# A windowed-attention block with a mixture of experts: the feed-forward's first product as seven block products, its other sums on other engines, and three seams in another order

## The chip, the cores and the metric

The kernel runs on one core of a Trainium2 chip. Five engines work side by side, each through its own queue in order: TensorE (PE, matmuls; PEld is its weight load), VectorE (DVE), ScalarE (ACT), GpSimd (POOL, which also issues the gathers by index) and SyncE (SP, which issues the other transfers). They meet through semaphores only. TensorE writes PSUM, of which the kernel keeps seven banks in one rotating pool and one bank apart. The metric is the time of one execution on the device in microseconds (us), as the median of several.

## The reference

Inputs are 4096 rows `x` of 256 numbers, and everything is float32. Cut to what matters (`LN` is a plain layer norm, biases are shown):

```python
xn   = LN(x)
# attention in windows of 64, 8 heads, each window sees itself and both neighbours
attn = window_attention(xn @ Wq + bq, xn @ Wk + bk, xn @ Wv + bv) @ Wo + bo
x1   = LN(xn + attn) * gamma + beta
mlp  = x1 + gelu(x1 @ W1 + b1) @ W2 + b2            # hidden width 1024
# mixture of experts: 8 experts, the two with the largest scores for each row
w    = top2_normalised(softmax(xn @ gate_w.T + gate_b))
moe  = sum_e w[e] * (silu((xn @ gp_w[e].T + gp_b[e]) * (xn @ up_w[e].T + up_b[e])) @ down_w[e].T + down_b[e])
out  = x + mlp + moe
```

## The kernel before

The whole program is one straight list of instructions: with `manual_schedule` every engine gets its instructions in the order in which the Python code emits them, and an engine whose next instruction waits holds everything behind it.

Stages, in order of time:

1. **Norm, scores, routing** (to about 75 us). The normed rows go to DRAM as `xnd`. Each row's two experts and its two places in the sorted list of (row, expert) pairs are worked out; `token` says which row belongs to each place, `slot` where each row's two results will lie.
2. **The main loop** `for b in range(ALWAYS)`, 34 rounds. Each round handles one *unit* of an expert's work (one or two tiles of 128 rows) and, in the first 32, one half of the heads for two tiles of the attention. A unit's rows come by `gather` (indirect transfers on GpSimd, L814), its weights by `load_gu` and `load_down` (SP, L214 and L222, 1670 KB and 896 KB). The expert's number is read from a table in SBUF: `expert_then`, a copy that GpSimd makes (L1326), for the units 0 and 1 once `gus` isn't empty, and `expert` otherwise. `turned` transposes the rows on TensorE (L827). The unit's results go to DRAM as `done` (L1003). In round `b == STEPS` (32) the attention's SBUF is given back, the feed-forward's weights `W1`, `W2` and the first two groups' inputs are loaded; in round 33 GpSimd makes `V2`, sums of blocks of `W2`; ScalarE's root and VectorE's few small steps make `r2` and `shift2` out of the second layer norm's moments, and `second_norm` (L1177) applies them to groups 0 and 1 late in the round.
3. **Late units** (to 850.72 us). Five more units may be needed or not; each lies in a `tc.If` on a flag (L1506), and `whole` computes it, with its copies from PSUM (`summed`, L985) at the end of the same branch. In this data three of the five run. Every engine goes through the branches, also those that have nothing in them.
4. **The feed-forward loop** `for g in range(NG)`, eight groups of 512 rows. `hidden(g)` makes x1 @ W1 on TensorE (L1210: eight banks of 512 columns, two products each) and ScalarE's Gelu out of PSUM into `hT` (L1217). `second(g - 1)`, one group behind, makes gelu(...) @ W2 out of seven products of blocks (L1281), with sums of hidden blocks (`sums_of_hidden`, VectorE, L1241 to L1245) and sums of weights (`V2`) as operands, and adds what comes out into `acc` on VectorE (L1291, L1301, L1309; u is ScalarE's copy of the first product, L1294). `turned2` transposes the next group's x1 (L1197) and ScalarE writes it to `x2T` (L1200). `second_base` puts x + beta + b2 + x2 * gamma into `acc` (VectorE, L1188 to L1190, 1024 wide). `picked` gathers the experts' results by row (L1255, eight transfers a group) and `combined` adds them to `acc`, weighted with `share` (VectorE, L1268, eight operations of 256). `store` writes `acc` out.

The seven products, here and below, are Winograd's form of Strassen's scheme: a product of 2 x 2 blocks with seven block products in place of eight, and fifteen block sums.

Of the kernel before, what the change touches and what calls it, by code (L numbers as in the profile page):

```python
# [103 lines left out]
def block_kernel(ctx: ExitStack, tc: tile.TileContext, a: dict, out: bass.AP):  # L104
# [24 lines left out]
    def bank(name):  # L129
        return psm.tile([P, G], F32, tag="bank", name=name)  # L130
# [873 lines left out]

    def whole(b, w, wd, xT, hT, banks, gss, y):

        _, n, _ = UNITS[b]
        n_in = n * P
        for k, f in enumerate([FCM] + list(range(FCM))):
            pb = halves(banks[k % 3])[:, :, 0:n_in]  # L1010
            gs = gss[k % 3][:, 0:n_in]
            if f == FCM:
                rest_of(w, xT, hT, pb, gs)
            else:
                chunk_of(f, w, xT, hT, pb, gs)
            if f == FCM:
                silu_rest(hT)
            elif f % 2:
                silu(hT, f - 1, f + 1)
        pds = [banks[k][:, 0:D] for k in (3, 1)[:n]]  # L1020
        results_rest(pds, wd, hT)
        results(pds, wd, hT)
        summed(y, pds)

# [140 lines left out]

    def second_loads(g):
        acc = accp.tile([P, TG, D], F32, tag="acc", name=f"acc{g}")
        x2 = accp.tile([P, TG, D], F32, tag="x2", name=f"x2_{g}", bufs=2)
        nc.sync.dma_start(out=x2, in_=rows(x1d, g * TG, TG))
        nc.sync.dma_start(out=acc, in_=rows(a["x"], g * TG, TG))  # L1170
        return acc, x2

# [12 lines left out]
    def second_base(g, acc, x2):  # L1185

        scaled = accp.tile([P, TG, D], F32, tag="scaled", name=f"scaled{g}", bufs=1)
        nc.vector.tensor_tensor(acc, acc, bcast(beta_b2, TG, 1), ALU.add)  # L1188
        nc.vector.tensor_tensor(scaled, x2, bcast(gamma, TG, 1), ALU.mult)
        nc.vector.tensor_tensor(acc, acc, scaled, ALU.add)  # L1190

# [12 lines left out]

    def hidden(g, x2T):
        hT = hf.tile([P, FC1, G], F32, tag="hf", name=f"hf{g}")
        for f in range(FC1):
            ph = bank(f"ph{g}_{f}")
            for c in range(DC):
                nc.tensor.matmul(  # L1210
                    ph,
                    W1[:, c, f * P : (f + 1) * P],
                    x2T[:, c, :],
                    start=(c == 0),
                    stop=(c == DC - 1),
                )
            nc.scalar.activation(hT[:, f, :], ph, AF.Gelu, bias=b1[:, f : f + 1])  # L1217
        return hT
# [30 lines left out]
    def picked(g):  # L1249

        ys = []
        for i in range(g * TG, (g + 1) * TG):
            for k in range(2):
                y = got.tile([P, D], F32, tag="got", name=f"got{i}_{k}")
                nc.gpsimd.indirect_dma_start(  # L1255
                    out=y,
                    out_offset=None,
                    in_=done,
                    in_offset=bass.IndirectOffsetOnAxis(ap=slot[:, k, i : i + 1], axis=0),
                )  # L1260
                ys.append(y)
        return ys

    def combined(g, acc, ys):
        for n, y in enumerate(ys):
            t, k = n // 2, n % 2
            i = g * TG + t
            nc.vector.scalar_tensor_tensor(  # L1268
                acc[:, t, :], y, share[:, k, i : i + 1], acc[:, t, :], ALU.mult, ALU.add
            )  # L1270

    def second(g, acc, hT, v):
# [31 lines left out]
        p5 = product(5, v[:, 0], V2[:, 0])  # L1304
        add(t1, C2, p5)
        add(t2, C2, p5)
        yield
        p7 = product(7, v[:, 2], V2[:, 2])
        nc.vector.tensor_tensor(u, p7, u, ALU.add)  # L1309
        add(t2, C1, u)  # L1310
        add(t2, C2, u)
        yield
# [10 lines left out]
    xs = {0: gather(0)}  # L1323
    res = {0: residual_load(0)}

    nc.gpsimd.tensor_copy(expert_then, expert)  # L1326
    downs[0], gus[1] = load_down(0), load_gu(1)
    xs[1] = gather(1)

# [24 lines left out]
    for b in range(ALWAYS):  # L1354
# [11 lines left out]
        if b == 0:  # L1366
            xT[0] = turned(0, xs.pop(0))
        if attends:
            pr, nm, sums = scores(i, hq)
            xd = apart(i, hq)  # L1370
# [40 lines left out]
        if b == STEPS:  # L1411
            att.close()
            wf = pool(ctx, "wf", right)
            accp = pool(ctx, "accp", right, bufs=4)
            V2 = wf.tile([P, 4, FC1 // 2, P], F32, tag="V2", name="V2")
            W1, W2 = matrix(wf, "W1", F1, DC), matrix(wf, "W2", D, FC1)
            b1 = column("b1", FC1, wf)
# [9 lines left out]
            for n in range(ALWAYS, BLOCKS):  # L1427
                xs[n] = gather(n)
            x2s = {n: second_loads(n) for n in range(2)}
        if b == STEPS + 1:  # L1430
            sums_of_weights()
            *_, r2 = rstd_of(mv2, root_of(mv2, NT, "b"), NT, "b")
            nc.vector.scalar_tensor_tensor(shift2, mv2[:, :, 0], -1.0, r2, ALU.mult, ALU.mult)
            nc.vector.tensor_tensor(beta_b2, beta, b2, ALU.add)
        if b == ALWAYS - 1:
# [3 lines left out]
        if b + 1 < ALWAYS:  # L1439
            xT[b + 1] = turned(b + 1, xs.pop(b + 1))  # L1440
        else:
            for n in range(ALWAYS, BLOCKS):
                xT[n] = turned(n, xs[n])
            for n in range(2):
                second_norm(n, x2s[n][1])
        g = b // TG
# [46 lines left out]

    x2Ts = {n: turned2(n, x2s[n][1]) for n in range(2)}

    for b in range(ALWAYS, BLOCKS):
        nc.gpsimd.memset(xs[b], 0.0)
    last = hTs[(ALWAYS - 1) % 2][:, :, 0 : UNITS[ALWAYS - 1][1] * P]
    pds = down_rest(ALWAYS - 1, downs[ALWAYS - 1], last)
    list(down(ALWAYS - 1, pds, downs.pop(ALWAYS - 1), last))  # L1500
    load_unit(ALWAYS + 2)
    for b in range(ALWAYS, BLOCKS):
        at, n, _ = UNITS[b]
        banks = [bank(f"whole{b}_{k}") for k in range(4)]
        gss = [he.tile([P, B], F32, tag="gs", name=f"gs{b}_{k}", bufs=3) for k in range(3)]
        with tc.If(flags[b] > 0):  # L1506
            whole(b, gus[b], downs[b], xT[b], hTs[b % 2][:, :, 0 : n * P], banks, gss, xs[b])
        load_unit(b + 3)

        nc.sync.dma_start(out=rows(done, at, n), in_=xs.pop(b))  # L1510

# [3 lines left out]
    hf = pool(ctx, "hf", right, bufs=2)  # L1515
    got = pool(ctx, "got", right, bufs=8)
    second_base(0, *x2s[0])
# [6 lines left out]
    for g in range(NG):  # L1524
        if g + 2 < NG:
            x2s[g + 2] = second_loads(g + 2)
        hT = hidden(g, x2Ts.pop(g))
        if g + 1 < NG:
            second_base(g + 1, *x2s[g + 1])
        if g > 0:  # L1530
            acc = x2s.pop(g - 1)[0]
            combined(g - 1, acc, ys)
        if 0 < g < NG - 1:
            x2Ts[g + 1] = turned2(g + 1, x2s[g + 1][1])
        if g + 2 < NG:
            second_norm(g + 2, x2s[g + 2][1])
        ys = picked(g)
        outs = second(g - 1, acc, *last) if g > 0 else iter(())
# [8 lines left out]
    acc = x2s.pop(NG - 1)[0]  # L1547
    combined(NG - 1, acc, ys)
    outs = second(NG - 1, acc, *last)
    some(outs, 6)  # L1550
    store(NG - 1, 0, 2, acc)
# [88 lines left out]
```

## Time and profile before

| | |
|---|---|
| runs | 1069.36, 1069.93, 1071.85 us; median 1069.93 us |
| profiled execution: its own time | 1071.19 us |
| profiled execution: span from first to last instruction | 1069.5 us |
| granted TensorE clock, mean | 0.998 |
| busy share of the span: PE, DVE, ACT, POOL | 99%, 70%, 54%, 55% |
| feed-forward loop, first matmul | 850.55 us (the chain counts it from 850.72) |
| one period of that loop, 945.79 to 972.91: PE, DVE, ACT, POOL busy | 27.12, 15.86, 9.05, 7.95 us of 27.12 |
| last operation on VectorE in the chain, then the last store | starts 1065.92, 0.42 us; span ends 1069.5 |

Times in all views are us from the start of the span. A line of a timeline has start, length, engine, line of the kernel, operation, and the tiles as written<-read; in brackets stands the idle time just before, and what ended it. In a table by groups of instructions a line ends with busy us, mean ns of one, and idle us before them.

### The profile page before, as it was taken

Reading aid. Unit: us, or ns where it says so; the run is one execution under the profiler, and the core shown is the slowest. Engines: PE = TensorE matmul, PEld = TensorE weight load, DVE = VectorE, ACT = ScalarE, POOL = GpSimd, SP = SyncE. Lnnn points to the kernel's source line nnn. Section 1 sums busy time; section 2 is a strip of 40 time slices with the busy share of each in tenths; the row PEclk is TensorE's granted clock in tenths of the full one; section 3 lists DMA queues with packets and bytes.
Section 4 is the critical chain, followed back from the end, with each engine's and each line's share of the span. In section 5 each row is a group of like instructions: output and inputs, shape, how many; then the busy total and the mean of one; then the engine's idle time right before and its main releaser. Section 6 shows DMA issues by size and latency. Waiting matters only on the chain. (4 is left out here: it accounts for less than half of the span.)

```text
span 1069.5 us, 20380 instructions
## 1 busy us (share of the span) xinstructions
PE 1057.4 (99%) x7278; PEld 860.8 (80%) x7278; DVE 753.9 (70%) x1852; ACT 572.6 (54%) x1329; POOL 587.8 (55%) x706
## 2 busy tenths in 40 slices
PE   9998999999999999999999999999999999999998
PEld 6577887887888888888888888888887757777778
DVE  6666876886787687788888988888532455555546
ACT  4526556656657556756675666566455353333320
POOL 5417766676576666676877777767520053222220
PEclk9999999999999999999999999999999999999999
DMA  8225434445345344544544444345584343333111
GB/s 287 75 102 204 139 129 173 172 150 180 118 143 183 129 146 165 199 139 143 177 175 139 176 158 181 138 167 173 187 310 145 123 137 114 99 99 96 63 60 40
DMA packets 61047, 158.67 MB, mean 148 GB/s; under 512 B 6576, under 2 KB 46896, under 8 KB 56208
## 3 DMA queue, kind: packets, MB, share of 16 engines
q1 hardware_dynamic: 53632, 139.33, 37.4%
q0 software_dynamic: 6480, 17.70, 5.2%
q8 instruction: 59, 0.97, 0.4%
q10 hardware_dynamic: 832, 0.30, 0.1%
q14 instruction: 44, 0.36, 0.1%
HBM read 135.43 MB, written 21.89 MB: 147 GB/s over the span
## 5 line engine op out<-in xcount | busy, mean ns | idle before, releaser
L839 PE MATMUL gu<-xsT,wg 128*128 128x256 f32 (+1 forms) x1632 | 364.4, 370 | 0.0
L839 PEld LDWEIGHTS gu<-xsT,wg 128*128 128x128 f32 x1632 | 290.0, 191 | 46.5 <-DVE nm L1047 8.6
L1255 POOL DMA_INDIRECT got<-done,slot x64 | 64.6, 1010 | 177.0 <-DVE acc L1268 106.8
L847 ACT ACTIVATE gs<-gu,wg 128x256 f32<-128x256 f32 (+1 forms) x204 | 92.2, 452 | 120.4 <-PE gu L839 116.0
L1074 POOL TENSOR_TENSOR pr<-pr 128x256 f32<-128x256 f32 x128 | 114.2, 892 | 67.0 <-ACT pr L1062 67.0
L848 DVE SCALAR_TENSOR_TENSOR hT<-gu,wg,gs 128x256 f32<-128x256 f32 (+1 forms) x204 | 91.9, 461 | 78.7 <-ACT gs L847 77.8
L1075 POOL TENSOR_TENSOR pr<-pr,ident 128x256 f32<-128x256 f32 x128 | 132.8, 1037 | 10.0
L1062 ACT ACTIVATE pr<-pr,nm 128x256 f32<-128x256 f32 x256 | 126.8, 497 | 1.0 <-ACT xsT L831 0.6
L1210 PE MATMUL ph<-x2T,W 128*128 128x512 f32 x256 | 111.0, 592 | 0.0
L1217 ACT ACTIVATE hf<-ph,b 128x512 f32<-128x512 f32 x64 | 43.9, 687 | 121.8 <-PE ph L1210 55.3
L1047 DVE CUSTOM_DVE_ANT_0 pr<-ps,mask 128x256 f32<-128x256 f32 x256 | 90.7, 421 | 16.6 <-PE ps L1033 16.6
L880 ACT ACTIVATE hT<-hT 128x512 f32<-128x512 f32 (+2 forms) x179 | 84.9, 485 | 32.5 <-DVE hT L848 22.4
L814 POOL DMA_INDIRECT xs<-xnd,token x71 | 69.0, 972 | 50.5 <-DVE paired_tiles L781 33.1
L1210 PEld LDWEIGHTS ph<-x2T,W 128*128 128x128 f32 x256 | 48.2, 190 | 57.9 <-issue 54.5
L1092 DVE TENSOR_TENSOR pr<-pr,rec 128x1024 f32<-128x1024 f32 x32 | 39.2, 1226 | 41.9 <-POOL pr L1074 41.9
L1105 POOL TENSOR_TENSOR xd<-xd,same 128x256 f32<-128x256 f32 x32 | 19.7, 617 | 83.7 <-DVE same L1103 83.5
L1291 DVE TENSOR_TENSOR acc<-u,acc 128x256 f32<-128x256 f32 x32 | 12.9, 423 | 68.7 <-ACT u L1294 68.1
L929 POOL TENSOR_TENSOR ts<-wd 128x384 f32<-128x384 f32 x54 | 54.1, 1001 | 2.1
L1062 ACT ACT_TABLE_LOAD x31 | 39.8, 1283 | 19.9 <-DVE nm L1047 19.9
L973 ACT COPY y<-sh 128x512 f32<-128x512 f32 x27 | 15.8, 586 | 61.4 <-PE sh L952 61.4
L1062 ACT ACTIVATION_READ_ACCUMULATOR pr<-pr,nm 128x1 f32 x256 | 48.3, 189 | 0.0
L952 PE MATMUL pe<-wd,hT 128*128 128x128 f32 x324 | 44.9, 275 | 0.0
(252 smaller groups left out, 2112.1 us busy)
## 6 DMA issues: line engine op xcount, KB each, us to landing
wg<-in_gate_up SPq DMA_DIRECT2D x37, 1670.5 KB, 7.1
wd<-in_down SPq DMA_DIRECT2D x37, 896.0 KB, 4.8
done<-y SPq DMA_DIRECT2D x30, 256.0 KB, 2.1
x<-in_x SPq DMA_DIRECT2D x8, 512.0 KB, 5.5
xnd<-xn SPq DMA_DIRECT2D x8, 512.0 KB, 5.2
res<-xnd SPq DMA_DIRECT2D x16, 256.0 KB, 2.9
x1d<-res SPq DMA_DIRECT2D x16, 256.0 KB, 2.2
x<-x1d SPq DMA_DIRECT2D x8, 512.0 KB, 4.6
```

Source lines behind the costliest of these rows:

```text
L814: nc.gpsimd.indirect_dma_start(out=x[:, t, :], out_offset=None, in_=xnd, in_offset=bass.IndirectOffsetOnAxis(ap=token[:, i : i + 1], axis=0),)
L839: nc.tensor.matmul(pb[:, k, :], w[:, lo : lo + P], xT[:, c, :], start=(c == 0), stop=(c == DC - 1),)
L847: nc.scalar.activation(gs, pb[:, 0, :], AF.Identity, bias=w[:, gb : gb + 1])
L848: nc.vector.scalar_tensor_tensor(hT[:, f, :], pb[:, 1, :], w[:, ub : ub + 1], gs, ALU.add, ALU.mult)
L880: nc.scalar.activation(hT[on, lo:hi, :], hT[on, lo:hi, :], AF.Silu)
L929: nc.gpsimd.tensor_tensor(out_, left_, right_, ALU.subtract)
L1047: nc.vector.tensor_tensor_reduce(out=pr[:, hh, j, :], in0=ps[hh][:, j, :], in1=mask[:, kinds[j], :], scale=-1.0, scalar=-LOWEST, op0=ALU.a ...
L1062: nc.scalar.activation(pr[:, hh, j, :], pr[:, hh, j, :], AF.Exp, bias=nm[:, j, hh : hh + 1], scale=-1.0, accum_out=sums[:, j, hh : hh + 1],)
L1074: nc.gpsimd.tensor_tensor(first, first, second, ALU.add)
L1075: nc.gpsimd.tensor_tensor(second, second, bcast(ident, 2, 1), ALU.mult)
L1210: nc.tensor.matmul(ph, W1[:, c, f * P : (f + 1) * P], x2T[:, c, :], start=(c == 0), stop=(c == DC - 1),)
L1255: nc.gpsimd.indirect_dma_start(out=y, out_offset=None, in_=done, in_offset=bass.IndirectOffsetOnAxis(ap=slot[:, k, i : i + 1], axis=0),)
```

## The change

It has four parts.

- **First product.** `hidden` makes, for each of four pairs of 128 hidden columns, seven products of 256 columns out of blocks of `W1` and `x2T` and their sums: `V1` (four sums of weight blocks, made once on GpSimd behind `V2`) and `x2s` (four sums of input blocks for each group, GpSimd). The seven results lie in four banks. ScalarE copies p1 into `q`, VectorE makes five sums into `hT`, and the Gelus work in place on `hT`, out of SBUF. Behind them stands one step of `weighted`.
- **Other sums.** `second_base` moves from VectorE to GpSimd, in pieces of 256. The weighting with `share` moves from VectorE's `combined` to ScalarE (`weighted`: two scalings behind each block of `hidden`), and `combined` becomes two sums of 1024. `picked` is called right behind `hidden`. In `second` two pairs of adds become one add each.
- **Rows and norms.** `gather(1)` moves ahead of the copy `expert_then` and the loads that read it. The rows x2 of groups 0 and 1 are loaded ahead of `W1`; root, `shift2`, `beta_b2` and `second_norm` for both move to the start of round 33.
- **Late units' copies.** A unit's copies out of PSUM and its store move into a branch of their own, `emptied`, which is emitted behind the next unit's `whole`; the same holds for the copies of the last unit of the main loop.

```diff
@@ late units
-    def whole(b, w, wd, xT, hT, banks, gss, y):
+    def whole_results(b, banks):
+        return [banks[k][:, 0:D] for k in (3, 1)[: UNITS[b][1]]]
+
+    def whole(b, w, wd, xT, hT, banks, gss):
...
         results(pds, wd, hT)
-        summed(y, pds)
+
+    def emptied(b, banks, y):
+        at, n, _ = UNITS[b]
+        with tc.If(flags[b] > 0):
+            summed(y, whole_results(b, banks))
+
+        nc.sync.dma_start(out=rows(done, at, n), in_=y)
+        yield
@@ second_base
-        nc.vector.tensor_tensor(acc, acc, bcast(beta_b2, TG, 1), ALU.add)
-        nc.vector.tensor_tensor(scaled, x2, bcast(gamma, TG, 1), ALU.mult)
-        nc.vector.tensor_tensor(acc, acc, scaled, ALU.add)
+        for t in range(TG):
+            a_, s_ = acc[:, t, :], scaled[:, t, :]
+            nc.gpsimd.tensor_tensor(s_, x2[:, t, :], gamma, ALU.mult)
+            nc.gpsimd.tensor_tensor(a_, a_, beta_b2, ALU.add)
+            nc.gpsimd.tensor_tensor(a_, a_, s_, ALU.add)
@@ hidden
+    def sums_of_first_weights():
+        m = blocks_of_first()
+        a11, a12, a21, a22 = m[:, 0, 0], m[:, 0, 1], m[:, 1, 0], m[:, 1, 1]
+        s1, s2, s3, s4 = (V1[:, k] for k in range(4))
+        nc.gpsimd.tensor_tensor(s1, a21, a22, ALU.add)
+        for out_, left_, right_ in ((s2, s1, a11), (s3, a11, a21), (s4, a12, s2)):
+            nc.gpsimd.tensor_tensor(out_, left_, right_, ALU.subtract)
+
+    def sums_of_inputs(g, x2T):
+        ts = turns.tile([P, 4, B], F32, tag="x2s", name=f"x2s{g}")
+        b11, b12, b21, b22 = x2T[:, 0, 0:B], x2T[:, 0, B:], x2T[:, 1, 0:B], x2T[:, 1, B:]
+        t1, t2, t3, t4 = (ts[:, k] for k in range(4))
+        for out_, left_, right_ in ((t1, b12, b11), (t2, b22, t1), (t3, b22, b12), (t4, b21, t2)):
+            nc.gpsimd.tensor_tensor(out_, left_, right_, ALU.subtract)
+        return x2T, ts
+
-    def hidden(g, x2T):
+    def hidden(g, x2T, ts, others):
         hT = hf.tile([P, FC1, G], F32, tag="hf", name=f"hf{g}")
-        for f in range(FC1):
-            ph = bank(f"ph{g}_{f}")
-            for c in range(DC):
-                nc.tensor.matmul(ph, W1[:, c, f * P : (f + 1) * P], x2T[:, c, :], ...)
-            nc.scalar.activation(hT[:, f, :], ph, AF.Gelu, bias=b1[:, f : f + 1])
+        w = blocks_of_first()
+        for m in range(FC1 // 2):
+            banks = [halves(bank(f"ph{g}_{m}_{k}")) for k in range(4)]
+            p1, p6, p7, p5, p2, p4, p3 = (banks[k // 2][:, k % 2, :] for k in range(7))
+            for to, left_, right_ in (
+                (p1, w[:, 0, 0, m, :], x2T[:, 0, 0:B]),
+                (p6, V1[:, 1, m, :], ts[:, 1]),
+                (p7, V1[:, 2, m, :], ts[:, 2]),
+                (p5, V1[:, 0, m, :], ts[:, 0]),
+                (p2, w[:, 0, 1, m, :], x2T[:, 1, 0:B]),
+                (p4, w[:, 1, 1, m, :], ts[:, 3]),
+                (p3, V1[:, 3, m, :], x2T[:, 1, B:]),
+            ):
+                nc.tensor.matmul(to, left_, right_, start=True, stop=True)
+
+            q = hf.tile([P, 3, B], F32, tag="q", name=f"q{g}_{m}")
+            both = hT[:, 2 * m : 2 * m + 2, :]
+            nc.scalar.copy(q[:, 0], p1)
+            nc.vector.tensor_tensor(q[:, 1], p6, q[:, 0], ALU.add)
+            nc.vector.tensor_tensor(q[:, 2], p7, q[:, 1], ALU.add)
+            nc.vector.tensor_tensor(both[:, :, B:], q[:, 1:3], bcast(p5, 2, 1), ALU.add)
+            nc.vector.tensor_tensor(both[:, :, 0:B], banks[2], q[:, 0::2], ALU.add)
+            nc.vector.tensor_tensor(both[:, 0, B:], p3, both[:, 0, B:], ALU.add)
+            for f in range(2 * m, 2 * m + 2):
+                nc.scalar.activation(hT[:, f, :], hT[:, f, :], AF.Gelu, bias=b1[:, f : f + 1])
+            next(others, None)
         return hT
@@ picked, combined
-                y = got.tile([P, D], F32, tag="got", name=f"got{i}_{k}")
+        ys = got.tile([P, 2, TG, D], F32, tag="got", name=f"got{g}")
...
-            nc.vector.scalar_tensor_tensor(
-                acc[:, t, :], y, share[:, k, i : i + 1], acc[:, t, :], ALU.mult, ALU.add
-            )
+    def weighted(g, ys):
+        for t in range(TG):
+            for k in range(2):
+                i = g * TG + t
+                nc.scalar.activation(
+                    ys[:, k, t, :], ys[:, k, t, :], AF.Copy, scale=share[:, k, i : i + 1]
+                )
+            yield
+
+    def combined(acc, ys):
+        for k in range(2):
+            nc.vector.tensor_tensor(acc, acc, ys[:, k], ALU.add)
@@ second
-        add(t1, C2, p5)
-        add(t2, C2, p5)
+        right = acc.rearrange("p (k t) d -> p k t d", k=2)[:, :, :, C2]
+        nc.vector.tensor_tensor(right, right, bcast(p5, 2, 1), ALU.add)
...
-        add(t2, C1, u)
-        add(t2, C2, u)
+        low = acc[:, t2, :].rearrange("p t (h n) -> p t h n", h=2)
+        nc.vector.tensor_tensor(low, low, bcast(u, 2, 2), ALU.add)
@@ rows
     res = {0: residual_load(0)}
+    xs[1] = gather(1)
     nc.gpsimd.tensor_copy(expert_then, expert)
     downs[0], gus[1] = load_down(0), load_gu(1)
-    xs[1] = gather(1)
@@ norms, at the start of round STEPS + 1 (before: behind its second chunk, second_norm behind the transposes)
+        if b == STEPS + 1:
+            *_, r2 = rstd_of(mv2, root_of(mv2, NT, "b"), NT, "b")
+            nc.vector.scalar_tensor_tensor(shift2, mv2[:, :, 0], -1.0, r2, ALU.mult, ALU.mult)
+            nc.vector.tensor_tensor(beta_b2, beta, b2, ALU.add)
+            for n in range(2):
+                second_norm(n, x2s[n][1])
@@ the late units
+    x2Ts = {n: sums_of_inputs(n, x2T) for n, x2T in x2Ts.items()}
...
-    list(down(ALWAYS - 1, pds, downs.pop(ALWAYS - 1), last))
+    made = down(ALWAYS - 1, pds, downs.pop(ALWAYS - 1), last)
+    next(made)
...
+        list(made)
+        made = emptied(b, banks, xs.pop(b))
         load_unit(b + 3)
-        nc.sync.dma_start(out=rows(done, at, n), in_=xs.pop(b))
+    list(made)
@@ the feed-forward loop
-        hT = hidden(g, x2Ts.pop(g))
+        hT = hidden(g, *x2Ts.pop(g), weighted(g - 1, ys) if g > 0 else iter(()))
+        ys_last = ys if g > 0 else None
+        ys = picked(g)
         if g + 1 < NG:
             second_base(g + 1, *x2s[g + 1])
-        if g > 0:
-            acc = x2s.pop(g - 1)[0]
-            combined(g - 1, acc, ys)
         if 0 < g < NG - 1:
-            x2Ts[g + 1] = turned2(g + 1, x2s[g + 1][1])
+            x2Ts[g + 1] = sums_of_inputs(g + 1, turned2(g + 1, x2s[g + 1][1]))
         if g + 2 < NG:
             second_norm(g + 2, x2s[g + 2][1])
-        ys = picked(g)
+        acc = x2s.pop(g - 1)[0] if g > 0 else None
+        if g > 0:
+            combined(acc, ys_last)
         outs = second(g - 1, acc, *last) if g > 0 else iter(())
@@ the last group
-    combined(NG - 1, acc, ys)
+    list(weighted(NG - 1, ys))
     outs = second(NG - 1, acc, *last)
-    some(outs, 6)
+    some(outs, 2)
+    combined(acc, ys)
+    some(outs, 4)
```

## The prediction

> **What bounds the kernel now.** I read the granted clock first (0.998), then the page, then the chain of work that ended last in order of time, then each engine's timeline over one period of the feed-forward loop and over the three seams. The chain:
>
> ```profile
> 918.68 13.74 PE ph L1210 x32
> 932.41 0.87 PE pt L1197 x8
> 933.29 12.51 PE s L1281 x112
> 945.79 13.73 PE ph L1210 x32
> ...
> 1040.88 25.02 PE s L1281 x224
> 1065.90 0.02 issue
> 1065.92 0.42 DVE acc L1291
> ```
>
> Columns: start, length (us), engine, tile, line. From 850.72 on TensorE alone carries the end: a period is 13.74 (`hidden`) + 0.87 (`turned2`) + 12.51 (`second`) = 27.12 us, without idle. From 850.72 to the end of the span are 1069.5 - 850.72 = 218.8 us; that is the number the change is held against. The other engines are slack there, and this is how one of them is ordered:
>
> ```profile
> 909.21 0.36 ACT L1294 COPY u<-s 128x256 f32<-128x256 f32 x1
> 920.48 0.69 ACT L1217 ACTIVATE hf<-ph,b 128x512 f32<-128x512 f32 x1 [10.91 <-issue]
> 922.15 0.69 ACT L1217 ACTIVATE hf<-ph,b 128x512 f32<-128x512 f32 x1 [0.98 <-PE ph L1210]
> ```
>
> Each Gelu waits for TensorE alone, and nothing on ScalarE waits behind VectorE. Ahead of the loop TensorE stands still at two places that the change touches (in brackets: idle time, releaser):
>
> ```profile
> 86.88 0.55 PE L827 MATMUL pts<-ident,xs 128*128 128x128 f32 x3 [2.92 <-DMA xs<-xnd,token]
> 806.84 1.03 PE L889 MATMUL pe<-wd,hT 64*128 64x256 f32 x4 [1.28 <-ACT hT L880]
> ```
>
> **TensorE's own part.** `hidden` had 16 products of 512 columns, in 32 instructions of 13.74 / 32 = 0.429 us. Now it has 4 blocks of 7 products of 256 columns, 56 instructions. Such instructions at L839 come 24 in 5.18 us (777.11 to 782.29), 0.216 each: 56 x 0.216 = 12.09 us a group, 3.02 a block. Taken alone, 8 x 1.65 = 13.2 us less. Weight loads (0.19 us at L1210) fit under 0.216.
>
> **The new queue on ScalarE.** This decides. In each block ScalarE copies p1 into q, VectorE runs five sums, ScalarE runs two Gelus and, from group 1 on, two scalings of gathered rows. The instruction order of the changed kernel puts the copy of the next block *behind* the Gelus of this one, and those wait for VectorE's fifth sum. So copy, sums, Gelus and scalings run one after the other, however early TensorE is. Prices:
>
> ```profile
> 912.87 0.42 DVE L1301 TENSOR_TENSOR u<-s,u 128x256 f32<-128x256 f32 x1
> 913.32 0.42 DVE L1291 TENSOR_TENSOR acc<-u,acc 128x256 f32<-128x256 f32 x1
> ...
> 760.66 0.68 DVE L1114 TENSOR_TENSOR pr<-pT,first_keys 128x512 f32<-128x512 f32 x1
> 761.26 0.68 DVE L1114 TENSOR_TENSOR pr<-pT,second_keys 128x512 f32<-128x512 f32 x1
> ...
> 808.16 0.63 ACT L880 ACTIVATE hT<-hT 128x512 f32<-128x512 f32 x1 [0.55 <-DVE hT L848]
> 808.70 2.77 ACT L1200 ACTIVATE x2T<-pt,beta_c,gamma_c 128x512 f32<-128x512 f32 x4
> ```
>
> Start to start: a 256-wide sum that the next needs 0.45, a 512-wide one 0.60, a 512-wide activation from SBUF 0.54. Handing over between the two engines takes 0.03 (808.13 to 808.16). Block: copy 0.36 + 0.03 + sums (0.45 + 0.45 + 0.60 + 0.60 + 0.42 = 2.52) + 0.03 + Gelus 1.08 + scalings 0.98 = **5.00 us**, against 3.02 on TensorE. A scaling (256 wide, SBUF, scale per partition) isn't in the trace: bounds are L847, 0.36 to the next, and L1177, 8 in 4.05 with a last one of 0.60, so 0.49; with its source in SBUF it is nearest to L1177, and I take 0.49.
>
> **From the last block to the next group.** Count from the end of the last block's fifth sum. ScalarE: Gelus and scalings start at 0.03, the two x2T writes at 2.09 (0.67 each, L1200), four norms at 3.43 (0.49 each, L1177), the copy of u at 5.39, done 5.75. VectorE: two 1024-wide `combined` sums end near 4.1, then it waits for u until 5.78. From there in its order: u and p2 into acc (0.45 + 0.34), s1, s2 (1.25 + 1.14), p6 (0.45 + 0.45), p5 (0.60), s3, s4 (1.14 + 1.14), p7 (0.45 + 0.60), p3, p4 (0.34 + 0.34): 8.69 us, from the same lines today (910.48 to 917.92). Only at 14.47 can the first sum of the next group start. TensorE isn't late: with seven banks in turn, four a block, each bank waits for the one seven places before it. The last product of block 3 needs what the first sum of block 2 frees, the first two products of `second` what blocks 2 and 3 free by -2.1, the others what is read by 3.6; at 1.79 a product (12.51 / 7) the last ends by about 8.7, ahead of its add.
>
> Moved to GpSimd: 12 sums of `second_base` and 4 of the inputs, 256 wide. L1074, L1075 run in 0.73 where nothing is in their way (82.64), so 16 x 0.73 = 11.7, plus 8 gathers at 1.25 (L1255, 0.95 and 0.30): 21.7 us a period, hidden under VectorE's chain. If that cover went, GpSimd would bind from 27.1 us on. But both engines meet:
>
> ```profile
> L940 DVE TENSOR_TENSOR hT<-hT 128x384 f32<-128x384 f32 x27 | 29.2, 1081 | 0.0
> ...
> L938 DVE TENSOR_TENSOR ss<-hT 128x384 f32<-128x384 f32 x27 | 15.0, 554 | 0.0
> ```
>
> Same width, both operands in SBUF; L940 runs against GpSimd's sums and takes 0.53 longer (L939, at 967 ns, 0.41). Here the four input sums meet `combined`, the sum of u, and s1: I place them one by one and get 0.9 us a period; bounds 0 (no meeting) and 4 x 0.73 = 2.9. In group 0 `second_base(1)` meets the four sums of the hidden block: 4 x 0.47 = 1.9 us.
>
> [...]
>
> Period: 2.52 + 3 x 5.00 + 14.47 + 0.9 = **32.9 us** against 27.12.
>
> **Sum over the loop.** Group 0 has no scalings, so blocks of 4.02. Its first fifth sum ends at 3.7 (p4 is there at 6 x 0.43 + 0.08 = 2.66, then 0.60 and 0.42), the table load for Gelu adds 1.28 once (L1217 today), the fourth ends at 17.0; Gelus to 18.2; sums 4.67 + 1.9; so group 1 starts at 24.8 and its last fifth sum is at 24.8 + 2.52 + 15.0 = 42.3. Six periods to group 7: 197.4, less 1.6 as group 6 has no norms ahead of u. At 238.1 begins the tail: VectorE's sums of `second(6)` to about 12.8, those of `second(7)`, with its two `combined` after the second product's, behind TensorE's last products (about 19) to 19.5, then what the last store takes today, 1069.5 - 1066.3 = 3.2. Total 260.8, or 42.0 more than 218.8.
>
> **Seams.** Rows: `gather(1)` goes ahead of the copy on GpSimd that releases `load_down(0)` and `load_gu(1)` on SP, so these start some 2.5 us later (two gathers at 1.25); `load_down(1)` behind them too. The wait of 2.92 goes, since `gather(0)`, without those loads beside it, was used by TensorE at most 2.0 us after its issue (76.44 to 78.45). What is late next is wd and wg of unit 1, used at 100.0, with 20 us in hand. Gain 2.9, bounds 0 and 2.9. Norms: root and eight norms move into ScalarE's gap of 7.27 us ahead of 794.60 and off the queue ahead of the silu that TensorE waited for: 1.28, less some stall where the banks of the next copies come free later; I take 1.0, bounds -0.5 and 1.28. SP brings the two x2 loads ahead of W1 and W2, due at 786 (V2) and 850. Late copies: TensorE passed from one taken unit to the next without a gap (weight loads to 831.03, next at 831.05), so no wait for copies is there to remove; each unit adds a branch. Between 0 and the 1.0 us that a skipped unit costs (840.24 to 841.23); five empty branches I take at 0, for the nearest row is the branch of a load, also empty on TensorE, which lies in that gapless passage. Seams together -3.9.
>
> Sum: 1069.5 + 42.0 - 3.9 = 1107.6 on the profiled span; the median of the runs, 1069.93, lies 0.4 above that span, so **1108 us**.
>
> **Rivals.** *TensorE stays the bound* (faster): the copy isn't held up, blocks follow at TensorE's 3.02. Same sums with 3.02: group 1's last fifth sum at 32.1, periods of 26.95, total 214.9, time 1069.5 - 3.9 - 3.9 = 1061.7; with VectorE's chain also overlapped, 1069.5 - 13.2 - 3.9 = 1052.4. It decides from a block spacing of 3.4 us down, as 24 spacings (three in each of eight groups) carry the 38 us of loss, 1.6 each. For it: TensorE at 99% today and VectorE busy 15.9 of 27.1 us a period. Against: the order of the two queues and the waits in it. 6%.
> *GpSimd meets VectorE far more* (slower still): 2.9 us a period in place of 0.9, scalings at 0.60 (+0.9 a period): 1108 + 12 + 5 = 1125. For it L940, against it that the block sums read PSUM with one operand, and L1160, such a sum, keeps 0.69 beside GpSimd. 12%.
> *The chain a little shorter*: scalings at 0.36 (-1.0 a period) and no meeting (-0.9, and -1.9 in group 0): 1092.8. This is the low end of the forecast's own range.
>
> **How the numbers follow.** Forecast 80%, own range 1093 to 1117 (upper end half of the second rival's addition). The 80% range reaches a little beyond: **1089 to 1122**, leaving out the first rival and the far end of the second. About 0.2% is what a measurement of this kernel can tell from no change. Faster 6%, same 2% (block spacing right at 3.4), slower 92%.
>
> **What would show it.** Right: in the profile after, TensorE has idle time in each group of the loop, released by VectorE or ScalarE at the new products; `q` copies about 5.0 us apart in groups 1 to 7 and 4.0 in group 0; periods near 33 us; TensorE's share well below 99% after 850 us; the chain that ended last runs through ScalarE and VectorE. The 2.92 and 1.28 us waits are gone and the loop starts near 847. Wrong: `q` copies about 3 us apart; or periods set by GpSimd's gathers and sums; or sums of 512 elements from PSUM much shorter than 0.60 with a broadcast operand. The prediction fails on the fast side if ScalarE's copy can pass a waiting Gelu.

## The result, and the profile after

| | before | after |
|---|---|---|
| median, us | 1070.49 (1069.36 to 1071.85, 4 runs) | 1112.01 (1111.85 to 1112.25, 4 runs) |
| profiled span, us | 1069.5 | 1110.5 |
| first product of the feed-forward loop, us | 850.55 | 846.97 |

The ratio is 1.0385, 95% interval [1.037, 1.04]: the change makes the kernel 41.5 us slower, where 1108 us had been forecast. Ahead of the loop it is 3.6 us faster, in the loop it loses 44.6: from the first product to the end of the span are 263.5 us, where there were 218.95.

The busy part and the slices of the page (busy tenths in 40 slices) of the kernel after:

```profile
PE 1059.6 (95%) x7470; PEld 895.3 (81%) x7470; DVE 800.0 (72%) x1924; ACT 605.4 (55%) x1425; POOL 695.3 (63%) x838
...
PE   9999999999999999999999999999999688888788
```

The same slices of the kernel before:

```profile
PE   9998999999999999999999999999999999999998
```

By the prediction's terms TensorE has 13.2 us less to do than in the kernel before, and yet it takes longer: from the 32nd slice on, where the loop runs, it stands still for 10 to 40% of the time. What it waited for, and what the others waited for, is the view of waits from 845 us to the end (us in total, times, longest):

```profile
ACT hf L1273 <- DVE hf L1271: 115.0, 31, 7.5
DVE q L1267 <- ACT q L1266: 58.6, 25, 3.0
...
PE ph L1262 <- DVE q L1267: 15.6, 13, 6.0
...
PE ph L1262 <- DVE u L1370: 9.6, 6, 1.9
```

ScalarE's Gelus (L1273) wait for VectorE's fifth sum, VectorE's first sum (L1267) waits for ScalarE's copy (L1266): the two engines wait for one another in turn, and TensorE for what VectorE hasn't emptied. Before, ScalarE's Gelus waited for TensorE in this loop (880 us to 1066 us):

```profile
ACT hf L1217 <- issue: 54.4, 5, 10.9
ACT hf L1217 <- PE ph L1210: 42.9, 42, 1.0
...
ACT hf L1217 <- DVE acc L1268: 12.1, 1, 12.1
```

For the first Gelus of five groups ("issue") the view names no releaser. The one wait there that it puts down to VectorE lies ahead of group 7's first Gelu, at 1028.95. TensorE starts that group's products at 1026.98, as far ahead of the Gelu as in the other groups, so it isn't shown that VectorE held it. The ring is seen best in ScalarE's timeline of group 3 (start, length, operation; in brackets the idle time before and its end):

```profile
946.15 1.33 ACT L1273 ACTIVATE hf<-hf,b 128x512 f32<-128x512 f32 x2 [2.68 <-DVE hf L1271]
947.39 0.89 ACT L1324 ACTIVATE got<-got,share 128x256 f32<-128x256 f32 x2
948.19 0.35 ACT L1266 COPY q<-ph 128x256 f32<-128x256 f32 x1
951.21 1.33 ACT L1273 ACTIVATE hf<-hf,b 128x512 f32<-128x512 f32 x2 [2.67 <-DVE hf L1271]
...
957.51 0.89 ACT L1324 ACTIVATE got<-got,share 128x256 f32<-128x256 f32 x2
958.31 1.42 ACT L1219 ACTIVATE x2T<-pt,beta_c,gamma_c 128x512 f32<-128x512 f32 x2
959.64 2.07 ACT L1194 ACTIVATE x<-x,shift,r_b 128x256 f32<-128x256 f32 x4
961.60 0.35 ACT L1355 COPY u<-s 128x256 f32<-128x256 f32 x1
```

and in VectorE's of the same group:

```profile
948.57 0.42 DVE L1267 TENSOR_TENSOR q<-ph,q 128x256 f32<-128x256 f32 x1 [2.45 <-ACT q L1266]
...
955.82 0.41 DVE L1271 TENSOR_TENSOR hf<-ph,hf 128x256 f32<-128x256 f32 x1
958.46 2.90 DVE L1331 TENSOR_TENSOR acc<-acc,got 128x1024 f32<-128x1024 f32 x2 [2.22 <-issue]
961.99 0.92 DVE L1352 TENSOR_TENSOR acc<-u,acc 128x256 f32<-128x256 f32 x1 [0.64 <-ACT u L1355]
...
971.34 0.41 DVE L1267 TENSOR_TENSOR q<-ph,q 128x256 f32<-128x256 f32 x1
```

Copy, sums, Gelus, scalings, then the next copy: from 948.19 to 953.25 (the next copy, left out above) one block takes 5.06 us, of which TensorE needs 3.02. The copy at 948.19 reads p1, which TensorE had written by 941.1; it starts where the scalings in front of it end. Behind the last block the copy of u comes only after the scalings, the x2T writes and the norms, and VectorE's tail (to 971.34) only after u. The first sums of groups 1 to 7 start at 872.76, 905.91, 938.45, 971.34, 1003.84, 1036.37 and 1068.94: a period is 32.7 us where it was 27.12. "issue" at 958.46 isn't free time: the bracket names no releaser, but ScalarE's scalings (957.51, done at 958.40) are what the sum needs.

The chain that ended last, which was TensorE's in the loop before, now is VectorE's, back to such an "issue":

```profile
1086.73 1.86 issue
1088.58 1.24 DVE acc L1331
...
1092.20 1.14 DVE hv L1298
...
1106.42 0.52 DVEq L1709
```

At the seams, TensorE's timeline of the kernel after has this in place of the idle 2.92 and 1.28 us:

```profile
84.19 0.60 PE L827 MATMUL pts<-ident,xs 128*128 128x128 f32 x4
84.63 5.35 PE L839 MATMUL gu<-xsT,wg 128*128 128x256 f32 x24
...
91.59 0.44 PE L1133 MATMUL pX<-ident,xd 128*128 128x128 f32 x2 [0.74 <-POOL xd L1115]
...
792.92 0.88 PE L827 MATMUL pts<-ident,xs 128*128 128x128 f32 x6 [0.52 <-DVE hT L848]
...
810.15 1.10 PE L856 MATMUL whole<-xsT,wg 128*128 128x256 f32 x4 [0.78 <-PEq L1574]
...
837.68 0.68 PE L856 MATMUL whole<-xsT,wg 128*128 128x128 f32 x4 [0.84 <-DVE xs L985]
```

Both waits are gone; 0.74 and 0.52 us of new ones stand for them. The first wait had cost more than its 2.92 us: the same 24 instructions (L839) that take 5.35 us here took 7.03 right behind it in the kernel before (at 87.26), where the clock granted from 88 to 92 us was 0.57, and 1.00 from 92 us on.

### The profile page after: what moved, and what is told of

Its sections match the earlier page's. It is cut to its first block, busy times and chain, and to the rows that moved or that the text cites. A ratio compares the mean times of both kernels' runs of the same rounds, so it can differ in the third digit from the quotient of the medians.

```text
span 1110.5 us, 21188 instructions
## 1 busy us (share of the span) xinstructions
PE 1059.6 (95%) x7470; PEld 895.3 (81%) x7470; DVE 800.0 (72%) x1924; ACT 605.4 (55%) x1425; POOL 695.3 (63%) x838
## 5 line engine op out<-in xcount | busy, mean ns | idle before, releaser
L839 PE MATMUL gu<-xsT,wg 128*128 128x256 f32 (+1 forms) x1632 | 362.8, 369 | 0.0
L839 PEld LDWEIGHTS gu<-xsT,wg 128*128 128x128 f32 x1632 | 288.8, 190 | 46.0 <-DVE nm L1057 9.0
L1273 ACT ACTIVATE hf<-hf,b 128x512 f32<-128x512 f32 x64 | 42.7, 714 | 115.0 <-DVE hf L1271 115.0
L1312 POOL DMA_INDIRECT got<-done,slot x64 | 67.6, 1056 | 48.0 <-DVE hf L1269 29.9
L1267 DVE TENSOR_TENSOR q<-ph,q 128x256 f32<-128x256 f32 x32 | 13.5, 422 | 58.6 <-ACT q L1266 58.6
L1262 PE MATMUL ph<-x2T,W 128*128 128x256 f32 x128 | 40.4, 398 | 15.9 <-DVE u L1370 9.6
L1262 PE MATMUL ph<-x2s,V 128*128 128x256 f32 x192 | 49.2, 390 | 0.0
L1243 POOL TENSOR_TENSOR x2s<-x2T 128x256 f32<-128x256 f32 x16 | 12.4, 773 | 55.0 <-ACT x2T L1219 55.0
```

What stands on the lines that cost most here:

```text
L839: nc.tensor.matmul(pb[:, k, :], w[:, lo : lo + P], xT[:, c, :], start=(c == 0), stop=(c == DC - 1),)
L1262: nc.tensor.matmul(to, left_, right_, start=True, stop=True)
L1312: nc.gpsimd.indirect_dma_start(out=ys[:, k, t, :], out_offset=None, in_=done, in_offset=bass.IndirectOffsetOnAxis(ap=slot[:, k, i : i + 1] ...
```

## The experiments

The kernels ran in four groups, each beside the kernel before on the same chip, whose medians there were 1072.3 to 1074.0 us; so ratios are compared, and where microseconds are named they are a ratio's distance from 1 times 1070.5.

| kernel | ratio to before | 95% interval |
|---|---|---|
| the change | 1.0385 | [1.037, 1.04] |
| copy_first | 1.0008 | [0.9997, 1.0019] |
| scaling_on_vector | 1.0182 | [1.0161, 1.0204] |
| base_on_vector | 1.048 | [1.0463, 1.0497] |
| old_first_product | 0.9977 | [0.9968, 0.9987] |
| seams_only | 0.9961 | [0.995, 0.9973] |
| gather_only | 0.9969 | [0.9957, 0.9981] |
| rows_only | 0.9998 | [0.999, 1.0007] |
| copy_first_pool_order | 1.0005 | [0.9996, 1.0015] |
| first_group_apart | 0.9999 | [0.9989, 1.0009] |
| base_ahead_of_loop | 0.9924 | [0.9909, 0.9939] |
| start_mended | 0.9916 | [0.9902, 0.9929] |
| norms_behind_copy | 0.9888 | [0.9868, 0.9909] |

**copy_first: the next block's copy ahead of this block's Gelus.** Nothing else is changed.

```diff
             nc.vector.tensor_tensor(both[:, 0, B:], p3, both[:, 0, B:], ALU.add)
-            for f in range(2 * m, 2 * m + 2):
-                nc.scalar.activation(hT[:, f, :], hT[:, f, :], AF.Gelu, bias=b1[:, f : f + 1])
-            next(others, None)
+            if m > 0:
+                gelus(m - 1)          # the two Gelus and next(others) of block m - 1
+        gelus(FC1 // 2 - 1)
```

> Only ScalarE's order in hidden changes: the copy of p1 of a block is issued ahead of the Gelus and scalings of the block before. Theory (the queue on ScalarE is the cause): block sums follow each other at VectorE's or TensorE's pace, 2.5 to 3.1 us in place of 5.06, the period of the loop falls from 32.6 us to between 25.4 (TensorE) and 27, and the time to 1056 to 1068 us. Rival (GpSimd's sums and their meetings with VectorE set the period): the period stays above 30 us and the time above 1090 us.

1.0008: 40 of the 41.5 us are gone with one change of order. From group 2 on the first sums of a group's blocks follow one another every 2.5 to 3.8 us, and the groups every 26.0 to 27.4 us. That settles the cause, the order of ScalarE's queue, against the rival. But it ends some 3 us above the range of the theory, so something else took over. GpSimd's timeline in this kernel:

```profile
944.60 1.71 POOL L1208 TENSOR_TENSOR acc<-acc,beta_b 128x256 f32<-128x256 f32 x1
946.39 1.59 POOL L1209 TENSOR_TENSOR acc<-acc,scaled 128x256 f32<-128x256 f32 x1
947.95 0.90 POOL L1243 TENSOR_TENSOR x2s<-x2T 128x256 f32<-128x256 f32 x1
948.93 1.59 POOL L1243 TENSOR_TENSOR x2s<-x2T,x2s 128x256 f32<-128x256 f32 x1
```

With the shorter period GpSimd's base sums end behind the last block, among VectorE's sums with two operands in SBUF, where a sum takes 1.6 to 1.7 us in place of 0.73; the input sums (L1243) queue behind them, and TensorE waited for these once for 1.4 us. A wait of 6.4 us at the start of group 1 stays as well.

**scaling_on_vector: the weighting back on VectorE** (eight `scalar_tensor_tensor` in `combined`, no scalings on ScalarE).

```diff
-        hT = hidden(g, *x2Ts.pop(g), weighted(g - 1, ys) if g > 0 else iter(()))
+        hT = hidden(g, *x2Ts.pop(g), iter(()))
-            nc.vector.tensor_tensor(acc, acc, ys[:, k], ALU.add)
+            nc.vector.scalar_tensor_tensor(acc[:, t, :], ys[:, k, t, :], share[:, k, i : i + 1], acc[:, t, :], ALU.mult, ALU.add)
```

> The change, but the gathered rows are weighted on VectorE as before (eight operations of 256), not on ScalarE behind each block. Theory (what stands in ScalarE's queue between two copies is paid in full): block spacing 4.26 as in group 0 in place of 5.06, VectorE's tail about 1 us shorter as u comes earlier, period about 29.2 us, time 1084 to 1092 us. Rival (VectorE's amount of work sets the period): 1.25 us more a period, about 1120 us.

1.0182, inside the theory's range once it is brought to the 1070.5 level (1090). VectorE's timeline:

```profile
938.95 0.42 DVE L1267 TENSOR_TENSOR q<-ph,q 128x256 f32<-128x256 f32 x1 [1.66 <-ACT q L1266]
...
943.22 0.42 DVE L1267 TENSOR_TENSOR q<-ph,q 128x256 f32<-128x256 f32 x1 [1.66 <-ACT q L1266]
```

A block now takes 4.27 us, 0.8 less, which is what two scalings had taken on ScalarE, although VectorE got eight weightings (4.96 us) in place of two sums (2.90). The period fell from 32.5 to 29.6 us: what is taken off the ring counts in every block, what is put beside it hardly at all.

**base_on_vector: the base of the residual sum back on VectorE.**

```diff
-        for t in range(TG):
-            a_, s_ = acc[:, t, :], scaled[:, t, :]
-            nc.gpsimd.tensor_tensor(s_, x2[:, t, :], gamma, ALU.mult)
-            nc.gpsimd.tensor_tensor(a_, a_, beta_b2, ALU.add)
-            nc.gpsimd.tensor_tensor(a_, a_, s_, ALU.add)
+        nc.vector.tensor_tensor(acc, acc, bcast(beta_b2, TG, 1), ALU.add)
+        nc.vector.tensor_tensor(scaled, x2, bcast(gamma, TG, 1), ALU.mult)
+        nc.vector.tensor_tensor(acc, acc, scaled, ALU.add)
```

> The change with the base of the residual sum (three sums of 128x1024, 1.22 us each in the profile of before) back on VectorE instead of twelve sums of 128x256 on GpSimd. Theory (the spacing of the blocks, 5.06 us, set by ScalarE's order of issue, is what costs; GpSimd's new work meets VectorE only in its cover): the 3.7 us fall into the 2.2 us that VectorE waits ahead of the combining sums, and what they add past it is about what the meetings with GpSimd cost: ratio to before 1.035 to 1.05. Rival (the two engines excluding one another is what costs): clearly below the change's 1.0385, 1.02 or less.

1.048, at the upper end of the theory and far from the rival: the meetings of these twelve sums with VectorE aren't what costs, and moving them to GpSimd was right in this kernel. The four input sums still meet VectorE here: its two combining sums took 3.43 us at 965.66, where they take 2.48 in the kernel after with GpSimd idle (1101.14). The combining sums started 3.85 us behind the start of the last fifth sum, where after the change it was 2.64: of the 3.5 us that they take (962.14 to 965.66), 1.2 came on top in each group, and the rest fell into the wait of 2.22 that stands above.

**old_first_product and seams_only.** The first keeps everything of the change but the seven products (`hidden` as before, with `weighted` in it); the second is the kernel before with the three seams.

```diff
@@ old_first_product, against the change
-            for to, left_, right_ in ((p1, ...), ...): nc.tensor.matmul(to, left_, right_, start=True, stop=True)
+            for c in range(DC):
+                nc.tensor.matmul(ph, W1[:, c, f * P : (f + 1) * P], x2T[:, c, :], start=(c == 0), stop=(c == DC - 1))
+            nc.scalar.activation(hT[:, f, :], ph, AF.Gelu, bias=b1[:, f : f + 1])
```

> The first product as before (16 products of 512 columns, Gelu out of PSUM, no sums for it); everything else of the change stays: second_base on GpSimd, scalings on ScalarE, the seams. Theory: TensorE sets a period of 27.1 us again and only the seams' gain is left, 1064 to 1069 us. Rival (the other moved sums cost the time): above 1085 us.

> The kernel before with the three seams alone. Theory: 2.9 us from the gather, 1.0 from the norms, nothing from the copies: 1066 to 1068 us, and the loop's first product at about 847. Rival (the added branches and later expert loads cost as much): 1069 us or more.

0.9977 and 0.9961, both in their theories' ranges. The seams are worth 4.2 us, 2.9 to 5.4 by the interval. The other sums on GpSimd and ScalarE, with the old product, cost some 1.7 us of that again (the intervals overlap, so this isn't shown to differ from nothing). So the 43.7 us from 0.9977 to 1.0385 come with the new first product alone.

**gather_only and rows_only: which seam.** Each is the kernel before with one edit.

```diff
@@ gather_only
+    xs[1] = gather(1)
     nc.gpsimd.tensor_copy(expert_then, expert)
     downs[0], gus[1] = load_down(0), load_gu(1)
-    xs[1] = gather(1)
@@ rows_only: x2 of groups 0 and 1 ahead of the weights
+            x2s = {n: second_rows(n) for n in range(2)}
             W1, W2 = matrix(wf, "W1", F1, DC), matrix(wf, "W2", D, FC1)
```

> The kernel before with one of the three seams alone: the rows of the second norm loaded ahead of the weights. From the prediction: 2.9 us less, ratio 0.9973; the three seams together gave 0.9961 [0.995, 0.9973]. Rival (the norms' place is what gave the time): 0.999 or more.

> The kernel before with gather(1) issued ahead of GpSimd's copy and the first loads of units, and nothing else: what the prediction called the rows' seam and priced at 2.9 us (rows_only moved the loads of x2 instead, which the prediction had under the norms). seams_only shows the wait of 2.92 us gone and a new one of 0.8 us at the first pX. Theory: 2.0 to 2.9 us less, ratio 0.9973 to 0.998. Rival (the loads that start later cost it again): 0.999 or more.

rows_only was a slip of the expectation: what the prediction called "rows" is the order of the gathers, not these loads. It shows only that the loads by themselves give nothing (0.9998). gather_only is the edit that was meant: 0.9969, or 3.3 us with an interval of 1.3 either way, so by the medians most of the seams' gain, and a little more than the theory. Its trace is 3.5 us ahead of the one before at L1157 (122.75 for 126.28) and 2.0 us at the loop's first product (848.6 for 850.55); where the rest goes isn't shown. Idle time of TensorE in its first rounds:

```profile
90.91 0.44 PE L1123 MATMUL pX<-ident,xd 128*128 128x128 f32 x2 [0.75 <-POOL xd L1105]
...
101.22 0.94 PE L952 MATMUL pe<-ts,hT 128*128 128x128 f32 x6 [0.25 <-POOL ts L929]
```

**Five steps from copy_first to a version that beats both kernels.** First GpSimd's order: base of group g first, half of the gathers, the input sums, the other gathers; and the norms behind the copy of u.

```diff
-    second_base(0, *x2s[0])
     last = None
...
+        if g > 0:
+            second_base(g, *x2s[g])
         hT = hidden(g, *x2Ts.pop(g), weighted(g - 1, ys) if g > 0 else iter(()))
-        ys = picked(g)
-        if g + 1 < NG:
-            second_base(g + 1, *x2s[g + 1])
+        ys, picks = picked(g)
+        some(picks, 2 if g > 0 else TG)
+        if g == 0:
+            second_base(0, *x2s[0])
         if 0 < g < NG - 1:
             x2Ts[g + 1] = sums_of_inputs(g + 1, turned2(g + 1, x2s[g + 1][1]))
+        some(picks, TG)
```

> copy_first (its groups 2 to 7 came every 26.0 to 27.4 us, with GpSimd's base sums ending behind the last block and the sums of the inputs queued behind them) with GpSimd's order changed: base of group g first, two of the four pairs of gathers, sums of the inputs, the other gathers; the norms of group g+2 behind the copy of u on ScalarE. Theory (GpSimd's queue is what remained of the loss): periods 25.5 to 26.0, ratio 0.994 to 0.998 (copy_first had 1.0008); group 1 keeps its long start (30.6 us). Rival (VectorE's own work, 22.5 us of 26.3, is the bound): the periods stay over 26.3, ratio 0.999 to 1.002.

1.0005: no gain, and neither side's reason. The periods did fall to 24.5 to 25.8 us from group 2 on, as the theory had it; what they gained was lost once, in a wait of 13.8 us of TensorE in group 1. Next, then, the sums of group 0's hidden values, which VectorE has ahead of group 1's blocks, were put behind them:

```diff
+        if g == 1:
+            sums = sums_of_hidden(0, first)
+            last = first, next(sums)
+            some(sums, 1)
```

> copy_first_pool_order, and the sums of group 0's hidden values (four of 1.22 us on VectorE, issued between the blocks of group 0 and of group 1) issued behind the blocks of group 1, where nothing needs them earlier. In copy_first the first sums of groups 0, 1 and 2 lie 22.8 and 30.6 us apart, 53.4 together; TensorE's own work of these two groups is 12.1 + 25.4 = 37.5. Theory (TensorE waits for banks that VectorE empties behind those sums): 6 to 10 us less than copy_first_pool_order, ratio 0.986 to 0.991, the fastest of all kernels here. Rival (the wait at the start is for the table load, the late units or the gathers): within 2 us of copy_first_pool_order.

0.9999: the theory of that wait is wrong, and the time is as the rival had it. ScalarE's timeline shows the right one:

```profile
864.06 1.33 ACT L1253 ACTIVATE hf<-hf,b 128x512 f32<-128x512 f32 x2 [4.33 <-DVE hf L1277]
873.02 2.07 ACT L1194 ACTIVATE x<-x,shift,r_b 128x256 f32<-128x256 f32 x4 [7.62 <-DMA x<-x1d]
875.00 0.61 ACT L1272 COPY q<-ph 128x256 f32<-128x256 f32 x2
```

The copies of group 1 (875.00) stand behind the norms of group 2 (873.02), which wait for a load of x. That load was issued at 868.7, when GpSimd's last sum that reads the same buffer, in the base of group 0, had ended; and this base stood behind eight gathers on GpSimd by the order of the experiment itself. Base 0 ahead of the loop again, as in the change, with and without the step before:

```diff
+    second_base(0, *x2s[0])
     last = None
...
-        if g == 0:
-            second_base(0, *x2s[0])
```

> copy_first_pool_order with the base of group 0 ahead of the loop again, as in the change. In copy_first_pool_order and first_group_apart it lay behind the first gathers on GpSimd (ended at 870); the load of x for group 2 waited for it, the norms of group 2 waited for the load (7.62 us of idle ScalarE), and the copies of group 1 stood behind the norms in ScalarE's queue: TensorE idle 13.8 and 10.0 us, once. Theory (that one wait hides the gain of the later groups): of the 13.8 us some 5 stay, for the four sums of group 0's hidden values still lie ahead of group 1's blocks on VectorE: 1071.3 - 9 = about 1062 us of span, ratio 0.990 to 0.994. Rival (the start is bounded by the gathers, which GpSimd issues from 851 to 861 whatever else): 0.998 or more.

> first_group_apart with the base of group 0 ahead of the loop, as in the change. Its groups 2 to 7 ran every 25.2 to 25.5 us, TensorE's own work (the prediction's 25.44). Theory: group 2's blocks start at 847.5 + 12.1 + 25.5 = 885 where they started at 900 in first_group_apart, so 1070.5 - 10 to 15 = 1055.5 to 1060.5 us of span, ratio 0.985 to 0.990, the fastest of all kernels here. Rival (the gathers bound the start): 0.998 or more.

0.9924 and 0.9916: that wait had hidden the gain. base_ahead_of_loop came as expected (a span of 1062.3 us, with 6.2 us of the wait left); start_mended, with 1063.5 us, stays 3 us above its range: the shift of group 0's sums makes no difference that these intervals can tell, for the norms (865.29 to 867.25 there) still lay ahead of the copies of group 1. The last step puts them behind the first block's Gelus of group 1:

```diff
+        if g == 1:
+            others = norm_then(2, others)      # four norms, then the scalings
```

> start_mended (1063.5 us of span) with the four norms of group 2 (2.06 us on ScalarE, ahead of the copies of group 1) issued behind the first block's Gelus of group 1. In start_mended VectorE waits 3.62 us for that copy, TensorE 2.2 and 0.9 us for VectorE, and the products after it run at 0.42 us a pass in place of 0.22 for some 4 us. Theory (ScalarE's order of issue once more): group 1's first sum comes 3 to 3.6 us earlier, TensorE's 3.1 us of waits and the slow products behind them go, span 1059 to 1061, ratio 0.987 to 0.990. Rival (VectorE, which has the sums of two groups' hidden values in group 1, takes it back ahead of group 2, where TensorE waited 2.2 us): span 1062.5 to 1064, ratio 0.991 or more.

0.9888, as the theory had it, with a span of 1057.9 us. Against start_mended that is 3.0 us by the medians, but the two intervals overlap a little. The traces show the gain more clearly: group 2's first sum starts at 893.62 and not at 897.60, and the clock granted from 872 to 876 us is 1.00 and not 0.77. TensorE's waits in the whole loop, 5.3 us in start_mended, are these:

```profile
PE ph L1268 <- DVE u L1380: 1.3, 1, 1.3
PE s L1352 <- DVE hv L1305: 1.1, 1, 1.1
PE ph L1268 <- DVE hf L1275: 0.9, 1, 0.9
```

The rival falls: VectorE's double load in group 1 costs 1.3 + 1.1 us, and it doesn't take the gain back. Against seams_only it is 0.0073 or 7.8 us less; the seven products save 13.2 us of TensorE's work. The waits above are 3.3 of the difference of 5.4; the rest, 2.1 us, is as much as the interval leaves open, and nothing here shows what takes it.

## Why the prediction was right

**TensorE's own product.** 3.02 us a block was forecast. Where nothing holds TensorE up, first products of blocks follow every 3.02 us (927.76, 930.78 in first_group_apart), and there the first products of groups 3 and 4 lie 25.47 us apart (927.76, 953.23). That is TensorE's work alone, and by the prediction's terms it is 12.09 + 0.87 + 12.51 = 25.47 too.

**The ring on ScalarE and VectorE.** 5.00 us forecast, 5.06 measured. Three terms were off: two Gelus take 1.24 us, not 1.08 (946.15 to 947.39), two scalings 0.80, not 0.98 (947.39 to 948.19), and the five sums 2.60, not 2.52 (948.57 to 951.17). That they nearly cancel is luck. In group 0, without scalings, they don't: 4.26 in place of 4.02.

**From the last block to the next group.** Copy of u done 5.75 us behind the last fifth sum (forecast) and 5.72 (measured: 956.23 to 961.95); next first sum at 15.37 with the meetings, and at 15.1. The meetings came out as priced, 0.9: the combining sums took 2.90 us for both where they take 2.48 when GpSimd is idle (1101.14), and the first sum of u 0.92 where it takes 0.42 (1091.24). A steady period is 32.5 us, forecast 32.9. The low end of the prediction's own range takes seven periods where its sum has six; with six it is 1094.7 and not 1092.8.

**The loop.** Group 1's last fifth sum ended at +44.2 us, forecast 42.3; from there to group 7's 195.6, forecast 195.8; the tail 23.8, forecast 22.7. The first and the last are the mis-sized terms. In the first, 0.4 is the first block's (its fifth sum ended at +4.1, forecast 3.7), 0.7 comes from group 0's three other blocks at 4.26, and 0.6 is a thing that the prediction had no term for: at the start of group 1 TensorE had stood still for 6 us, its next products took about twice as long (the granted clock was 0.69 from 865 to 880 us), and the sums waited for them, so that the first two blocks lie 5.67 us apart (872.76, 878.43). TensorE's timeline of the kernel after:

```profile
866.61 0.59 PE L1262 MATMUL ph<-x2s,W 128*128 128x256 f32 x2
873.23 1.22 PE L1262 MATMUL ph<-x2T,V 128*128 128x256 f32 x2 [6.02 <-DVE q L1267]
...
876.18 2.76 PE L1262 MATMUL ph<-x2s,V 128*128 128x256 f32 x6
```

Six instructions (three products) take 2.76 us there and 1.46 elsewhere. The tail has 0.6 us more of `second(6)` on VectorE, 0.1 of `second(7)` and 0.4 ahead of the end of the span.

**Seams.** -3.9 forecast, -4.2 measured with seams_only; in the trace of the change the loop began at 846.97, forecast 847, which is 3.6 earlier. The gathers' part was priced at 2.9 and measured 3.3. The number is right partly by luck, for the prediction counted the wait alone: in the traces 2.92 of wait and 1.68 of slower products behind it (7.03 less 5.35) go, and 0.74 of new wait comes. For the norms the 1.28 us of wait went and 0.52 came, 0.76 in place of 1.0. The late copies, priced at nothing, show 0.78 and 0.84 us ahead of two late units where there were 0.71 and 0.62, so 0.3 us lost.

**Rivals.** That TensorE stays the bound needed the copy ahead of the Gelus, and copy_first shows both that the order alone forbade it and that this order wasn't enough for it: GpSimd's order and the start of the loop were next. That GpSimd meets VectorE far more didn't come about, for GpSimd's base sums fell among VectorE's waits and its block sums, which read PSUM with one operand, until copy_first shortened that time. Beside block sums they keep their time: 0.72 us at 944.37, next to a VectorE sum of 0.69 at 944.49.

**Where GpSimd's sums meet VectorE's.** In the kernel after, where sums with two operands in SBUF ran on both engines at once (866.63 to 872.84), GpSimd's 0.73 us became 1.58 to 1.73, some 0.9 more, and of VectorE's four sums of 1.22 the first kept its time and the others took 1.63 to 1.74, 0.4 to 0.5 more. So GpSimd bore more there than a whole instruction of its own, VectorE less than half of one of its. The price on VectorE is what the rows of before had shown (0.41 and 0.53 at L939 and L940). The second rival's 2.9 us a period, 12 in the loop, isn't shown in the kernel after: a period's meetings cost VectorE the 0.9 above.

## What to carry to other kernels

When a step gets a new producer (here Gelus fed by VectorE in place of TensorE), walk the queue of its engine: everything that is issued behind it now waits for the new producer too, and a single early copy behind it closes a ring that no busy share shows (here 5.06 us a block where TensorE needs 3.02, with ScalarE busy for 55% of the span and VectorE for 72%; the copy's place alone took back 40 of the 41.5 us). Issue the instruction that starts the next round ahead of those that end this one. When a wait is removed and the gain doesn't come, look for a single long wait at the start of the loop before doubting the steady state: here a single wait of 13.8 us hid what the later periods had won.

## What the runs showed of the hardware that was not expected

- **A short stall can slow TensorE's next products.** Behind waits of 6.0 to 13.8 us the granted clock was 0.50 for the first microseconds of work: in copy_first, where TensorE had waited 6.4 us, the stretches 868 to 872, 872 to 876, 876 to 880 and 880 to 884 have 0.94, 0.50, 0.71 and 1.00; in the kernel after, behind 6.0 us, and in first_group_apart, behind 10.0, it is 0.50 from 872 to 880; in copy_first_pool_order, behind 13.8, from 872 to 884. Shorter waits do it at times. Behind the 2.92 us of the kernel before 24 instructions took 7.03 us in place of 5.35; behind 2.21 us in start_mended (896.27) six instructions took 2.38 in place of 1.46, with a clock of 0.72 from 896 to 900. But behind 2.19 us in first_group_apart (904.95) the clock from 904 to 908 was 1.00, behind 1.91 us in the kernel after (970.08) six instructions took 1.66, and behind 1.32 us in norms_behind_copy (892.29) 1.73. So the length of a wait of about 2 us doesn't decide it. In finer slices the clock was back at 1.00 from 91.6 in the kernel before, 4.7 us behind the first product after the wait (86.88), and from 881.0 in the kernel after, 7.8 us behind it (873.23).
- **A gather's issue can be stretched too.** GpSimd's issue of one gather (L1312) took 0.95 us, but 1.80 at 963.64 in the kernel after, and 1.91 in copy_first at 954.50, each beside a VectorE sum with two operands in SBUF. Not every one beside such a sum is: in the kernel after the gather at 967.00 kept 0.95, with a sum of VectorE (L1301) from 967.34 on.
